# The last 64 features of the q/k/v products in float32r parts, and MLP weight rows split by ScalarE and GpSimd

## The chip, the cores and the metric

The kernel runs on one core of one Trainium2 chip. The metric is the device time of one execution in microseconds (us), read from the hardware; the kernel before took 3217.29 us (median of 3 runs, 3215.63 to 3218.51). The engines of the core are TensorE (PE in the profile; its weight loads are the row PEld), VectorE (DVE), ScalarE (ACT), GpSimd (POOL) and SyncE (SP), which only issues DMAs here. Each engine takes its instructions in one order; they meet through semaphores.

## The reference

One transformer block with conditioning, on x of 2 x 2048 x 576 in float32, with 16 heads of 36 and an MLP of 2304:

```python
mod = silu(c) @ w_ada + b_ada
sh_msa, sc_msa, g_msa, sh_mlp, sc_mlp, g_mlp = split(mod, 6, axis=1)
xn = ln(x, 1e-6) * (1 + sc_msa) + sh_msa
q, k, v = split(xn @ w_qkv + b_qkv)        # 576 -> 3 x 576
q, k = ln(q, 1e-5), ln(k, 1e-5)            # per head
o = softmax(q @ k.T * 36**-0.5) @ v
x = x + g_msa * (o @ w_proj + b_proj)
xn2 = ln(x, 1e-6) * (1 + sc_mlp) + sh_mlp
return x + g_mlp * (gelu(xn2 @ w1 + b1) @ w2 + b2)
```

The width of 576 matters for this change: it is four chunks of 128 rows and one of 64.

## The kernel before

The program first looks at the gains and biases of the head norms and then takes one of two branches; with these inputs it runs `block_of_small`. That branch goes through these stages, once for each of the two batches where not said otherwise:

1. **Inputs** (`inputs`, batch 0 from about 19 us, batch 1 from about 1110 us). For each of 16 tiles of 128 tokens: normalize the rows (`rows_normed`), turn them by five TensorE transposes (L357, L358), scale and shift them into `xnt` (L365), multiply by the weights of q, k and v, add the bias, normalize per head, and turn the result by nine transposes (L938) into `qo` and `kr`.
2. **Attention** (`attend`, L1073 and L1086 on TensorE, L1077 on ScalarE).
3. **Output projection** (`outputs`, from about 1038 us for batch 0 and 2121 us for batch 1). In the second of these, work for the MLP is laid between the tiles: `between` says at which tile t a piece is called. The pieces are the loads of the first token tiles, their norms, their transposes and shifts (`block_modulated`), and the preparation of w1.
4. **MLP**, first product (`whole_part` L1445, `last_part` L1459) and second product (L1610).

The q, k and v products each have two halves of 288 columns. A half is four matmuls with 128 rows (`whole`, L400) and one with 64 rows (`halved`, L411). The 64-row matmuls of the two halves sit in rows 0 to 63 and 64 to 127, so they run side by side; the transposed tail holds its 64 features twice, and `last_chunk` loads the weight rows accordingly. For most tiles the order on TensorE is q whole, transposes of the next tile, k whole, then three pairs of 64-row matmuls together, v whole, and the transposes by feature of two tiles ago. The last two tiles of a batch use `two_products`, which alternates the order of the two kinds.

The MLP's first product already treats its last 64 features differently. `last_modulated` writes the tail as a float32r part (L382), the tail in full (L383), and on GpSimd their difference (L384); `weight_parts` does the same to the weight rows on VectorE, with the high part in rows 0 to 63 and the remainder in rows 64 to 127 (L394, L395). Two float32r matmuls with all 128 rows (L1459), one for each part of the tokens, then give the product.

In the second output projection GpSimd's queue also issues the DMAs of the residual rows: `residual` loads a tile (L1178) and `summed` stores one (L1191). A load into one of the nine scratch tiles has to wait until the store of the tile that used it before is done. The w1 load of 4.7 MB (L1351) is issued by SyncE at the start of this stage.

TensorE's order is written out by hand throughout, VectorE's in the input stage, in attention and from the second output projection on, GpSimd's in attention. Elsewhere a scheduler sets the order when the program is built.

Of the kernel before, what the change touches and what calls it, by code (L numbers as in the profile page):

```python
# [8 lines left out]
F32 = mybir.dt.float32  # L9
F32R = mybir.dt.float32r  # L10
I32 = mybir.dt.int32
AF = mybir.ActivationFunctionType
# [19 lines left out]
def dit_block(  # L32
# [342 lines left out]

    def affine(which, k, b):
        return dict(bias=mod[:, which, k, b : b + 1], scale=mod[:, which + 1, k, b : b + 1])
# [8 lines left out]
    def modulated_parts(dst, cols, t4, t1, which, b):  # L386

        last_modulated(dst, cols, t1, which, b)
        for k in range(FULL):
            nc.scalar.activation(dst[0][:, k, cols], t4[:, k * P : (k + 1) * P], AF.Identity, **affine(which, k, b))  # L390

    def weight_parts(dst, src):

        nc.vector.tensor_copy(dst[0:64], src)  # L394
        nc.vector.tensor_tensor(dst[64:128], src, dst[0:64].bitcast(F32), ALU.subtract)  # L395
# [350 lines left out]
    def block_of_small():  # L746
# [10 lines left out]
        close_xs = token_tiles(5)  # L757
# [88 lines left out]
        def input_weights(then=lambda t: None):  # L846
            pool, close = opened("wq")
            wq = pool.tile([P, FULL, 3 * C], F32, name="wq")
            wq4 = pool.tile([P, 3, HALF], F32, name="wq4")
            bq = pool.tile([P, 3 * C], F32, name="bq")  # L850
            for f0, n in ((0, HALF), (HALF, HALF), (C, C), (2 * C, C)):
                f = slice(f0, f0 + n)
                nc.sync.dma_start(out=wq[:, :, f], in_=w_qkv[0:512, f].rearrange("(k p) f -> p k f", p=P))
                if f0 == HALF:
                    last_chunk(wq4, w_qkv, 3, HALF)
                if f0 == C:
                    then(1)
                    nc.sync.dma_start(out=bq, in_=b_qkv.partition_broadcast(P))
                    then(2)
            return (wq, wq4, bq), close  # L860
# [13 lines left out]
        def input_by_feature(b, rows, apart=False):  # L874
            xnt = xs["pool"].tile([P, NKC, P], F32, name="xnt", bufs=2)
            modulated(xnt, rows, 0, b, apart)
            return xnt

        def first_modulated():
            xnt = xs["pool"].tile([P, NKC, P], F32, name="xnt", bufs=2)  # L880
            for k in range(NKC):
                nc.scalar.activation(  # L882
                    xnt[:, k, :],
                    x_first[:, k * P : (k + 1) * P],
                    AF.Identity,
                    bias=mod[:, 0, k, 0:1],
                    scale=mod[:, 1, k, 0:1],
                )
            return xnt

        def inputs(b, weights, work, xnt, loaded):
# [75 lines left out]
            def next_rows(t):  # L967
                return tile_normed(loaded.pop(0)) if loaded else input_rows(b, t, nc.sync)

            def product(w, xnt):  # L970

                ps = s_tile()
                return ps, (
                    [ps[:, a, :HALF] for a in range(2)],
                    lambda k, a: xnt[:, k, :],
                    lambda k, a: (
                        wq[:, k, w * C + a * HALF : w * C + (a + 1) * HALF] if k < FULL else wq4[:, w, :]
                    ),
                )
# [16 lines left out]
            for t in range(NT - 2):  # L996
# [3 lines left out]
                q, q_parts = product(0, xnt)  # L1000
                whole(*q_parts, True)
                behind = b == t == 0
                if behind:
                    k, k_parts = product(1, xnt)
                    whole(*k_parts, True)
# [3 lines left out]
                rows = next_rows(t + 2)  # L1009
                if not behind:  # L1010
                    k, k_parts = product(1, xnt)
                    whole(*k_parts, True)
                v, v_parts = product(2, xnt)
                halved(*q_parts, False)
                halved(*k_parts, False)
                halved(*v_parts, True)
                biased(0, q, t, both)
# [3 lines left out]
                whole(*v_parts, False)  # L1021
# [7 lines left out]
            for t in range(NT - 2, NT):  # L1029
                both = work.tile([P, 2 * C], F32, name="both", bufs=3)  # L1030
                for w in range(3):
                    ps, parts = product(w, xnt)
                    two_products(*parts, 3 * t + w)
# [316 lines left out]
        for i, (k, f) in enumerate(((0, 0), (0, 1), (1, 0), (1, 1))):  # L1350
            nc.sync.dma_start(  # L1351
                out=wb[:, i],
                in_=w1[k * PAIR : (k + 1) * PAIR, f * MH : (f + 1) * MH].rearrange("(k p) f -> p k f", p=P),
            )
        weight_sums = [
            lambda: weight_parts(wr[0], last_rows[:, 0]),
            lambda: weight_parts(wr[1], last_rows[:, 1]),
            lambda: nc.vector.tensor_tensor(last_rows[:, 1], last_rows[:, 1], last_rows[:, 0], ALU.subtract),
            lambda: weight_parts(wr[2], last_rows[:, 1]),
# [25 lines left out]
        for i, t in enumerate((6, 7, 8, 9, 10, 11, 12, 14)):  # L1385
            between.setdefault(t, []).append(weight_sums[i])
        in_order = tc.manual_schedule(engines={mybir.EngineType.DVE})
# [310 lines left out]
```

## Time and profile before

| | |
|---|---|
| median of 3 runs | 3217.29 us |
| the profiled execution, its own time | 3216.58 us |
| its span, first to last instruction | 3214.8 us |
| TensorE busy | 3192.7 us, 99% of the span |
| ScalarE, VectorE, GpSimd busy | 1509.1, 1459.6, 369.1 us |
| weight loads | 1904.6 us, beside the matmuls |
| mean granted TensorE clock | 0.999 |

Durations and gaps in the text are from this one execution. A float32 matmul leaves two records on TensorE and a float32r matmul one, so "x16" of L400 is eight matmuls. The records of consecutive matmuls overlap; what one costs is read from start to start. In the timeline a row is: start in us from the beginning of the span, length in us, engine, line, operation, tiles written and read, shape, count, and in brackets how long the engine was idle before it and what ended that.

### The profile page before, as it was taken

Reading aid. Unit: us, or ns where it says so; the run is one execution under the profiler, and the core shown is the slowest. Engines: PE = TensorE matmul, PEld = TensorE weight load, DVE = VectorE, ACT = ScalarE, POOL = GpSimd, SP = SyncE. Lnnn points to the kernel's source line nnn. Section 1 sums busy time; section 2 is a strip of 40 time slices with the busy share of each in tenths; the row PEclk is TensorE's granted clock in tenths of the full one; section 3 lists DMA queues with packets and bytes.
Section 4 is the critical chain, followed back from the end, with each engine's and each line's share of the span. In section 5 each row is a group of like instructions: output and inputs, shape, how many; then the busy total and the mean of one; then the engine's idle time right before and its main releaser. Section 6 shows DMA issues by size and latency. Waiting matters only on the chain.

```text
span 3214.8 us, 47053 instructions
## 1 busy us (share of the span) xinstructions
PE 3192.7 (99%) x18143; PEld 1904.6 (59%) x18143; DVE 1459.6 (45%) x2137; ACT 1509.1 (47%) x2984; POOL 369.1 (11%) x464
## 2 busy tenths in 40 slices
PE   8999999999999999999999999999999999999999
PEld 6774333333333777633333333358888888777777
DVE  4674333333333367633333333345555444455454
ACT  2335666666666033466666666633555552000000
POOL 2111000112110111200001111011000000111111
PEclk9999999999999999999999999999999999999999
DMA  4102212223221401121222223144322223333321
GB/s 132 30 26 68 75 33 69 64 72 86 71 81 34 145 23 31 30 54 44 48 47 67 65 69 75 44 160 166 121 88 91 95 80 128 136 133 111 118 103 38
DMA packets 129172, 252.86 MB, mean 79 GB/s; under 512 B 22947, under 2 KB 68460, under 8 KB 126828
## 3 DMA queue, kind: packets, MB, share of 16 engines
q1 hardware_dynamic: 105428, 181.78, 18.6%
q0 software_dynamic: 22640, 66.23, 7.4%
q8 instruction: 145, 2.38, 0.3%
q10 hardware_dynamic: 872, 1.77, 0.2%
q14 instruction: 87, 0.71, 0.1%
HBM read 135.11 MB, written 66.35 MB: 63 GB/s over the span
## 4 chain that ended last, share of the span: by engine, by line
PE 98%; DMA 1%; DVE 0%; SPq 0%; issue 0%; ACT 0%; POOL 0%; DVEq 0%; POOLq 0%
PE b L1086 28%; PE b L1073 19%; PE s L1610 15%; PE s L400 15%; PE m L1445 12%; PE m L1459 2%; PE s L411 2%; PE one L1445 2%; PE s L938 1%; PE s L357 0%; PE t L1505 0%; DMA wq<-in_w_qkv_dram 0%; DMA x_dram<-x 0%; PE b L192 0%; PE b L938 0%
## 5 line engine op out<-in xcount | busy, mean ns | idle before, releaser
L1077 ACT ACTIVATE pt<-b 128x512 f32<-128x512 f32 x2048 | 1057.7, 610 | 485.3 <-PE b L1086 272.2
L1086 PE MATMUL b<-pt,vt 128*64 128x512 f32 x4096 | 935.0, 599 | 0.0
L1086 PEld LDWEIGHTS b<-pt,vt 128*64 128x64 f32 x4096 | 272.0, 136 | 581.8 <-issue 439.2
L1073 PE MATMUL b<-qm,km 32*128 32x512 f32 x4096 | 566.9, 614 | 0.2 <-DMA km<-qo 0.2
L1134 DVE TENSOR_TENSOR ot<-b,ot 128x512 f32<-128x512 f32 x192 | 132.8, 692 | 652.9 <-PE b L1086 652.5
L1073 PE MATMUL b<-qe,ke 16*128 16x512 f32 x2048 | 423.1, 790 | 0.0
L400 PE MATMUL s<-wq,xnt 128*128 128x288 f32 x1536 | 391.4, 409 | 1.2 <-ACT xnt L882 0.8
L1610 PE MATMUL s<-ws,as 128*128 128x288 f32 x1440 | 351.8, 406 | 0.0
L1073 PEld LDWEIGHTS b<-qm,km 32*128 32x128 f32 x4096 | 191.8, 185 | 269.1 <-ACT pt L1077 207.0
L400 PEld LDWEIGHTS s<-wq,xnt 128*128 128x128 f32 x1536 | 285.1, 190 | 85.4 <-issue 13.5
L1610 PEld LDWEIGHTS s<-ws,as 128*128 128x128 f32 x1440 | 274.1, 190 | 75.1
L1105 DVE RECIPROCAL den<-den 128x512 f32<-128x512 f32 x64 | 213.6, 3337 | 10.8 <-DMA den<-den_dram 10.8
L1445 PE MATMUL m<-s,wb 128*128 128x256 f32 x864 | 210.1, 380 | 0.2 <-DVE s L1415 0.2
L1445 PE MATMUL m<-xnt,wb 128*128 128x256 f32 x864 | 210.2, 379 | 0.0
L1132 DVE COPY ot<-b 128x512 f32<-128x512 f32 x64 | 44.3, 692 | 334.7 <-PE b L1086 334.7
L1445 PEld LDWEIGHTS m<-s,wb 128*128 128x128 f32 x864 | 164.4, 190 | 22.5 <-DVE s L1415 0.6
L1073 PEld LDWEIGHTS b<-qe,ke 16*128 16x128 f32 x2048 | 108.3, 184 | 114.2 <-issue 112.8
L1445 PEld LDWEIGHTS m<-xnt,wb 128*128 128x128 f32 x864 | 159.1, 190 | 18.7
L1472 DVE TENSOR_TENSOR cs<-m,cs 128x512 f32<-128x512 f32 x72 | 49.8, 691 | 215.8 <-PE m L1459 207.1
L1610 PE MATMUL s<-ws,hidden 128*128 128x288 f32 x576 | 142.3, 406 | 0.0
L1588 DVE TENSOR_TENSOR as<-hidden 128x1152 f32<-128x1152 f32 x80 | 139.2, 1803 | 0.0
L400 PE MATMUL s<-wp,qo 128*128 128x288 f32 x512 | 127.8, 410 | 0.0
(182 smaller groups left out, 2573.9 us busy)
## 6 DMA issues: line engine op xcount, KB each, us to landing
gelu<-cs SPq DMA_DIRECT2D x144, 256.0 KB
hidden<-gelu SPq DMA_DIRECT2D x16, 2304.0 KB
den<-den_dram SPq DMA_DIRECT2D x128, 128.0 KB
x_dram<-kr POOLq DMA_DIRECT2D x48, 288.0 KB, 2.8
qm<-qo SPq DMA_DIRECT2D x192, 64.0 KB
kr<-in_x_dram POOLq DMA_DIRECT2D x32, 288.0 KB, 3.8
xr<-x_dram SPq DMA_DIRECT2D x32, 288.0 KB
out_dram<-y POOLq DMA_DIRECT2D x30, 288.0 KB, 3.8
```

What stands on the lines that cost most here:

```text
L400: nc.tensor.matmul(outs[a], stationary(k, a), moving(k, a), start=(first and k == 0), stop=(not first and k == FULL - 1),)
L411: nc.tensor.matmul(outs[a], stationary(FULL, a)[r], moving(FULL, a)[r], start=first, stop=not first)
L1073: nc.tensor.matmul(ps, k[r, keys], q[r, :], start=first, stop=not first)
L1077: nc.scalar.activation(pt[:, h, :], banks[2 * c + h], AF.Exp, scale=SCALE)
L1086: nc.tensor.matmul(acc[64 * h : 64 * h + 64, :], vt[:, v0 : v0 + 64], pt[:, h, :], start=pt is pts[0][0], stop=pt is pts[-1][0],)
L1105: nc.vector.reciprocal(den, den)
L1134: nc.vector.tensor_tensor(ot, acc, ot, ALU.add)
L1445: nc.tensor.matmul(out_m[m], wb[:, slot[m], k, f * P : (f + 1) * P], moving[m](k), start=k == 0 and m in (1, 2, 5, 6), stop=k == 1 and m == 1,
L1459: nc.tensor.matmul(out_m[m], wr[w][:, f * P : (f + 1) * P], a[:, i, t * PAIR : (t + 1) * PAIR], start=False, stop=i == 1 and m != 2,)
L1472: nc.vector.tensor_tensor(cs[:, 0:5:4, :], two(1), cs[:, 4:5, :].to_broadcast([P, 2, PAIR]), ALU.add)
L1588: nc.vector.tensor_tensor(stationary[m], x_, y_, op)
L1610: nc.tensor.matmul(ms[m], stationary[m][:, f, :], ws[m][:, f, :], start=(f == 0), stop=(f == HF - 1))
```

## The change

In the input stage the 64-row pairs go. `xnt` becomes a tuple of a tile with the four full chunks, a float32r tile with two parts, and a tail; each half of a product is now four float32 matmuls followed by two float32r matmuls with 128 rows. `product` runs both halves at once, so that q, k and v are each completed before the next begins, and the biases follow at once. The tail's weight rows are loaded into the first 64 rows of `bq`, split from there by VectorE, and only then is the bias loaded into `bq`. The parts of the tail are written after the four full chunks instead of before them. The pool of token tiles shrinks from five to four.

For the MLP, the split of w1's last rows moves: ScalarE makes the copy and GpSimd the subtraction, also of the sum of the two column halves. The four sums of `wb` stay on VectorE. They are called at tiles 6, 8, 10 and 12 instead of 10, 11, 12 and 14, and the pieces on the other two engines at 7, 9, 11 and 13 instead of 6 to 9.

```diff
+    def part_tiles(pool, cols, **bufs):
+        return (
+            pool.tile([P, FULL, cols], F32, name="xnt", **bufs),
+            pool.tile([P, 2, cols], F32R, name="xnt4", **bufs),
+            pool.tile([P, P], F32, name="tail", bufs=1),
+        )
...
     def modulated_parts(dst, cols, t4, t1, which, b):
-        last_modulated(dst, cols, t1, which, b)
         for k in range(FULL):
             nc.scalar.activation(dst[0][:, k, cols], t4[:, k * P : (k + 1) * P], AF.Identity, **affine(which, k, b))
-
-    def weight_parts(dst, src):
-        nc.vector.tensor_copy(dst[0:64], src)
-        nc.vector.tensor_tensor(dst[64:128], src, dst[0:64].bitcast(F32), ALU.subtract)
+        last_modulated(dst, cols, t1, which, b)
+
+    def weight_parts(dst, src, subtract=None):
+        if subtract is None:
+            nc.vector.tensor_copy(dst[0:64], src)
+        else:
+            nc.scalar.copy(dst[0:64], src)
+        (subtract or nc.vector).tensor_tensor(dst[64:128], src, dst[0:64].bitcast(F32), ALU.subtract)
...
-        close_xs = token_tiles(5)
+        close_xs = token_tiles(4)
...
-            wq4 = pool.tile([P, 3, HALF], F32, name="wq4")
+            wq4 = pool.tile([P, 3 * C], F32R, name="wq4")
...
                 if f0 == HALF:
-                    last_chunk(wq4, w_qkv, 3, HALF)
+                    nc.sync.dma_start(out=bq[0:64, :], in_=w_qkv[512:576, :])
+                    weight_parts(wq4, bq[0:64, :])
...
         def input_by_feature(b, rows, apart=False):
-            xnt = xs["pool"].tile([P, NKC, P], F32, name="xnt", bufs=2)
-            modulated(xnt, rows, 0, b, apart)
+            xnt = part_tiles(xs["pool"], P, bufs=2)
+            t4, t1 = transposed(*rows, apart)
+            modulated_parts(xnt, slice(0, P), t4, t1[:, :P], 0, b)
             return xnt
...
             def product(w, xnt):
                 ps = s_tile()
-                return ps, (
-                    [ps[:, a, :HALF] for a in range(2)],
-                    lambda k, a: xnt[:, k, :],
-                    lambda k, a: (
-                        wq[:, k, w * C + a * HALF : w * C + (a + 1) * HALF] if k < FULL else wq4[:, w, :]
-                    ),
-                )
+                full, parts, _ = xnt
+                for a in range(2):
+                    f = slice(w * C + a * HALF, w * C + (a + 1) * HALF)
+                    out_a = ps[:, a, :HALF]
+                    for k in range(FULL):
+                        nc.tensor.matmul(out_a, full[:, k, :], wq[:, k, f], start=k == 0, stop=False)
+                    for i in range(2):
+                        nc.tensor.matmul(out_a, parts[:, i, :], wq4[:, f], start=False, stop=i == 1)
+                return ps
...
-                q, q_parts = product(0, xnt)
-                whole(*q_parts, True)
+                q = product(0, xnt)
                 behind = b == t == 0
                 if behind:
-                    k, k_parts = product(1, xnt)
-                    whole(*k_parts, True)
+                    k = product(1, xnt)
                 ahead = input_by_feature(b, rows, t in ((0, 9), (0, 1))[b])
                 rows = next_rows(t + 2)
+                biased(0, q, t, both)
                 if not behind:
-                    k, k_parts = product(1, xnt)
-                    whole(*k_parts, True)
-                v, v_parts = product(2, xnt)
-                halved(*q_parts, False)
-                halved(*k_parts, False)
-                halved(*v_parts, True)
-                biased(0, q, t, both)
+                    k = product(1, xnt)
                 biased(1, k, t, both)
                 if t > 0:
                     head_scale(t - 1, before)
-                whole(*v_parts, False)
+                v = product(2, xnt)
                 biased(2, v, t, both)
...
+        left, right = last_rows[:, 0], last_rows[:, 1]
+        last_parts = [
+            lambda: weight_parts(wr[0], left, nc.gpsimd),
+            lambda: weight_parts(wr[1], right, nc.gpsimd),
+            lambda: nc.gpsimd.tensor_tensor(right, right, left, ALU.subtract),
+            lambda: weight_parts(wr[2], right, nc.gpsimd),
+        ]
         weight_sums = [
-            lambda: weight_parts(wr[0], last_rows[:, 0]),
-            lambda: weight_parts(wr[1], last_rows[:, 1]),
-            lambda: nc.vector.tensor_tensor(last_rows[:, 1], last_rows[:, 1], last_rows[:, 0], ALU.subtract),
-            lambda: weight_parts(wr[2], last_rows[:, 1]),
             lambda: nc.vector.tensor_tensor(wb[:, 4], wb[:, 1], wb[:, 0], ALU.subtract),
...
-        for i, t in enumerate((6, 7, 8, 9, 10, 11, 12, 14)):
+        for i, t in enumerate((6, 8, 10, 12)):
             between.setdefault(t, []).append(weight_sums[i])
+            between.setdefault(t + 1, []).append(last_parts[i])
```

More of the change, by code (lines that the diff above doesn't have):

```diff
@@ L874, in input_by_feature @@
         def input_by_feature(b, rows, apart=False):
-            xnt = xs["pool"].tile([P, NKC, P], F32, name="xnt", bufs=2)
-            modulated(xnt, rows, 0, b, apart)
+            xnt = part_tiles(xs["pool"], P, bufs=2)
+            t4, t1 = transposed(*rows, apart)
+            modulated_parts(xnt, slice(0, P), t4, t1[:, :P], 0, b)
             return xnt
         def first_modulated():
[L880 to L887, printed above, removed]
-                )
+            xnt = part_tiles(xs["pool"], P, bufs=2)
+            modulated_parts(xnt, slice(0, P), x_first[:, :512], x_first[:, 512:], 0, 0)
             return xnt
@@ L972, in product @@
                 ps = s_tile()
-                return ps, (
-                    [ps[:, a, :HALF] for a in range(2)],
-                    lambda k, a: xnt[:, k, :],
-                    lambda k, a: (
-                        wq[:, k, w * C + a * HALF : w * C + (a + 1) * HALF] if k < FULL else wq4[:, w, :]
-                    ),
-                )
+                full, parts, _ = xnt
[7 more added lines that the diff above has]
+                return ps
             def biased(w, ps, t, both):
@@ L1031, in inputs @@
                 for w in range(3):
-                    ps, parts = product(w, xnt)
-                    two_products(*parts, 3 * t + w)
+                    ps = product(w, xnt)
                     biased(w, ps, t, both)
```

## The prediction

> **What bounds the kernel now.** I read the page's chain first: work on TensorE all the way.
>
> ```profile
> PE 98%; DMA 1%; DVE 0%; SPq 0%; issue 0%; ACT 0%; POOL 0%; DVEq 0%; POOLq 0%
> ```
>
> So the change counts where it alters TensorE's work or makes it wait. Next, the timeline of one token tile in the input stage, TensorE alone:
>
> ```profile
> 118.50 4.15 PE L400 MATMUL s<-wq,xnt 128*128 128x288 f32 x16
> 122.49 1.15 PE L938 MATMUL s<-ident,both 128*128 128x128 f32 x9
> 123.47 4.05 PE L400 MATMUL s<-wq,xnt 128*128 128x288 f32 x16
> 127.35 0.60 PE L357 MATMUL s<-ident,xt 128*128 128x128 f32 x4
> 127.79 0.27 PE L358 MATMUL s<-ident,xt 128*128 128x128 f32 x1
> 127.90 4.05 PE L400 MATMUL s<-wq,xnt 128*128 128x288 f32 x16
> 131.88 1.73 PE L411 MATMUL s<-wq,xnt 64*128 64x288 f32 x12
> 133.53 1.24 PE L400 MATMUL s<-wq,xnt 128*128 128x288 f32 x4
> ```
>
> Start to start, without a gap: 133.53 - 118.50 = 15.03 us per tile. A float32 record of 288 columns costs 3.88/16 = 0.2425 us (123.47 to 127.35). The three 64-row pairs take 1.65 us where two records each make 3 x 0.485 = 1.455, and the L400 blocks on either side of them take 3.98 and 3.99, not 3.88: some 0.4 us per tile goes at the borders between 128-row and 64-row matmuls. Then the nearest rows for the new operations, in the MLP's first product:
>
> ```profile
> 2226.20 1.03 PE L1445 MATMUL m<-s,wb 128*128 128x256 f32 x4
> ...
> 2227.06 1.03 PE L1445 MATMUL one<-xnt,wb 128*128 128x256 f32 x4
> 2227.74 1.30 PE L1459 MATMUL m<-parts,wr 128*128 128x256 f32 x8
> 2228.88 0.27 PE L1505 MATMUL t<-ident,xt 128*128 128x128 f32 x1
> ```
>
> Four float32 records take 0.86 us; from 2227.06 to 2228.88 are 1.82, so the eight float32r matmuls take 0.96, 0.120 each, and no border shows. Last, the timeline of the second output projection, where the moved pieces stand:
>
> ```profile
> 2151.93 0.54 POOL L1178 DMA_DIRECT2D x<-x_dram  x1 [8.87 <-DMA x_dram<-x]
> ...
> 2155.26 0.29 ACT L276 ACTIVATE std<-mv,eps 128x1 f32<-128x1 f32 x1 [3.40 <-DVE mv L274]
> ...
> 2157.18 0.60 PE L357 MATMUL s<-ident,xt 128*128 128x128 f32 x4
> ...
> 2161.22 0.54 POOL L1178 DMA_DIRECT2D x<-x_dram  x1 [5.76 <-DMA x_dram<-x]
> ...
> 2163.89 0.46 ACT L383 ACTIVATE tail<-s,mod 128x128 f32<-128x128 f32 x1 [5.51 <-POOL parts L384]
> ...
> 2171.10 1.12 PE L357 MATMUL s<-ident,xt 128*128 128x128 f32 x4 [3.32 <-DVE product L1183]
> ...
> 2181.07 0.60 PE L357 MATMUL s<-ident,x_first 128*128 128x128 f32 x4
> ```
>
> GpSimd's queue stands still for DMA stores, ScalarE's behind it, and TensorE loses 3.3 us at 2171.
>
> **What the skill says.** The Trainium skill, "TensorE: Matmul & The Clock Gate", section "Back-to-back issue gap", gives N/2.4 + 2.5 ns for a warm matmul: 122.5 ns at 288 columns; the trace's 0.120 at 256 columns is above its 109. The same page, "What's actually happening", says that an idle TensorE falls to half clock for some 3.4 us: after the gap at 2171.10 the same 5 transposes and 32 records take 9.97 us to the next start, where 0.545 + 32 x 0.2425 = 8.31 are due; so 1.66 us is lost. "Architectural detail" on that page calls ScalarE's and VectorE's queues strict FIFO, as the 5.51 us above show. "GPSIMD Engine Reference", section "Elementwise — side-by-side cycle accounting", has 4497 ns for a two-input operation on 2048 elements; the trace's L1166 takes 1416 ns for 576 and L384 452 for 128, 2.15 ns per element.
>
> **The input stage.** Removed per tile: 1.455 us of 64-row pairs and 0.4 of borders. Added: 12 float32r matmuls. I take 0.122 each, the skill's figure and half a float32 record; the low end is the measured 0.120, the high end 0.133, should the 13 ns by which 0.120 exceeds 256 columns at 0.2425/576 per column be fixed. New tile: 48 x 0.2425 = 11.64, 14 transposes 1.53 (0.98 + 0.55), 1.46, and 0.03 for handing back to float32: 14.66, a gain of 0.37. For 27 tiles: 10.0. The last two tiles of a batch take 29.99 (228.66 to 258.65; 1318.11 to 1348.10) and need 96 x 0.2425 + 23 x 0.109 + 24 x 0.122 + 0.06 = 28.8: 1.2 per batch, 2.4. That leaves batch 0's first tile. VectorE is free at 19.4; the split of 64x1728 scales from L394 (744 ns at 1152) and L395 (1351) to 1.04 + 1.95, so the parts exist at 22.5. TensorE, starting at 18.90, wants them at 20.84 and waits 1.7. From there 0.24 + 1.94 + 0.24 (q), 4.37 (k), 0.55, 4.37 (v): the next tile starts at 34.2. Before, it is also 34.2, after waits for weights at 23.45 and 30.31. The bias load now waits for the split, and v's weights stand behind it on SP: 0.885 + 1.18 MB at 397 GB/s from 23.5 are there at about 29.5, needed at 29.9. No gain, and 0 to 1 us of loss; I take 0.3. Sum: **-12.1 us**, or -7.7 at 0.133.
>
> At nothing I cost: one more shift on ScalarE and a 0.45 us subtraction on GpSimd per tile (a tile's parts are wanted over 11 us after its transposes, ScalarE is busy 53 of 155 us there, and in the built order the subtraction stands before the scaling L928 of its iteration); four token tiles instead of five (a load may still start about two tiles ahead); the split for batch 1 (3 us on VectorE, whose next eviction TensorE awaits some 8 us later; without that cover, up to 3 us).
>
> **The second output projection.** VectorE loses 3 x (0.74 + 1.35) + 1.34 = 7.6 us, hidden but for part of the 3.3 us. What counts is where the built program puts the pieces. GpSimd: load x1_2 (the one at 2161.22), subtraction for wr1, load x1_3, difference of the halves, a store, the first tail subtraction. ScalarE: the copies for wr0 and wr1 before the first tile's square root, and the copy for wr2 **before the second tile's square root** (the one at 2155.26). That copy needs the difference, which needs GpSimd past the load at 2161.22. Behind the square root wait VectorE (its norm, then evictions) and TensorE's transposes of 2157.18. So: 2161.22 + 0.54, + 2.65 (1152 elements: 1416 + 576 x 2.15), + 0.54, + 2.65 = 2167.6; copy 1.16 (L913 has 1152 ns for that length); root 0.3; reciprocal, scaling and hops 0.9: transposes at 2170.0, 12.8 us late. With 1.7 of slow clock: +14.5. The old stall then goes, for the evictions are long ready: -(3.38 + 1.66) = -5.0. Net **+9.5 us**. Ends: GpSimd at L928's 2.13 us gives +8.5; at 1.84 times the price, the worst of L1593 (2607 for 576), +14; nothing or less only if that store lands 13 us sooner, while w1's 4.7 MB hold the DMA engines (DMA share 1.02 from 2140 to 2160). The copies for wr0 and wr1 delay the first tile's root by about 5 us; TensorE has about that much slack, and the later wait covers the rest.
>
> **Sum.** Against the profiled execution's 3216.6: -12.1 + 9.5 = 3214.0. It lies 0.7 below the median, so 3214.7 as a median; -2.6 us. No change means within 0.2%, 6.4 us, which is about what a measurement of this kernel can tell.
>
> **Rivals.**
> *The stall is hidden* (0.15): stores return sooner, the difference is ready early, and only the input stage and the old stall's end count: 3217.3 - 12.1 - 5 = 3200; half hidden, 3207. For it: DMA times are the least certain link. Against it: the load of w1 is untouched.
> *Slower, by the float32r matmuls* (0.17): row L1459 of the page is 91.0 us for 576, 158 ns each. Should they cost that when they alternate with float32 in twos, the stage gains 384 x 0.036 = 13.8 less, that is loses 1.7, and with the stall the time is 3217.3 + 1.7 + 9.5 = 3228. It decides at 0.129 each: above that the kernel is slower than before. Against it: 91.0 includes overlap with the float32 matmul ahead, and the starts give 0.120. For it: no trace shows pairs of them with 288 columns.
> *A second pass*: float32r of 288 columns at the float32 record's 0.2425 would cost 46 us, 3261 (0.03); L1459 speaks against it.
>
> **How the numbers follow.** Both effects as worked out: 0.65, 3209 to 3221. Faster 0.2 is the hidden stall and 0.05 of the forecast's tail, slower 0.2 the two dearer float32r prices, same the other 0.6. The range, 3205 to 3224, takes in 0.133 with the dear GpSimd price (3217.3 - 7.7 + 14 = 3223.6) and a stall half hidden (3207).
>
> **What would show it.** Tiles of the input stage 14.66 us apart without a 64-row matmul; TensorE waiting about 1.7 us at 21 us; in the second output projection a TensorE gap of some 13 us before the second tile's transposes, ScalarE's copy for wr2 released by GpSimd, and no gap at the third. It is wrong if tiles are over 14.8 us apart, if other gaps of a microsecond open in the input stage, or if that gap is under 8 or over 17 us.

## The result, and the profile after

The changed kernel takes 3226.47 us (median of 8 runs, 3225.47 to 3228.88), the kernel before beside it 3217.47 (8 runs, 3215.63 to 3218.51): a ratio of 1.003, 95% interval 1.0019 to 1.0041. It is 9.0 us slower; the prediction had it 2.6 us faster, and the time lies 2.5 us above the end of its range. The profiled execution took 3225.47 us with a span of 3223.7, 8.9 longer than before's 3214.8, so one pair of traces can be set against each other. TensorE still carries the chain of the page, but less of it:

```profile
PE 96%; DVE 1%; DMA 1%; issue 0%; ACT 0%; SPq 0%; POOL 0%; DVEq 0%; POOLq 0%; ACTq 0%
```

The stages, each from TensorE's first matmul of it to that of the next, in us:

| stage | before | after | difference |
|---|---|---|---|
| up to the first product | 18.90 | 20.04 | +1.14 |
| inputs, batch 0 | 239.76 | 237.96 | -1.80 |
| attention, batch 0 | 779.02 | 780.32 | +1.30 |
| output projection, batch 0 | 72.04 | 72.04 | 0 |
| inputs, batch 1 | 238.40 | 233.90 | -4.50 |
| attention, batch 1 | 772.75 | 772.95 | +0.20 |
| output projection, batch 1 | 79.12 | 91.74 | +12.62 |
| MLP, both products | 1014.82 | 1014.73 | -0.09 |

The input side was to bring 12.1 us and brought 3.7; the second output projection was to cost 9.5 and cost 12.6.

First the timeline of a token tile in the input stage, TensorE alone, half of v first:

```profile
119.19 2.10 PE L984 MATMUL s<-wq,xnt 128*128 128x288 f32 x8
120.91 0.64 PE L986 MATMUL s<-wq,xnt 128*128 128x288 f32 x2
121.39 2.10 PE L984 MATMUL s<-wq,xnt 128*128 128x288 f32 x8
...
133.47 0.65 PE L986 MATMUL s<-wq,xnt 128*128 128x288 f32 x2
133.96 1.37 PE L984 MATMUL s<-wq,xnt 128*128 128x288 f32 x5
```

The same place one tile later is 14.77 us on (119.19 to 133.96), not 14.66. A half takes 121.39 - 119.19 = 2.20; eight float32 records at 0.2425 are 1.94, so two float32r matmuls take 0.265, 0.1325 each.

The start of batch 0, TensorE alone before the change:

```profile
18.90 4.12 PE L400 MATMUL s<-wq,xnt 128*128 128x288 f32 x16 [0.76 <-ACT xnt L882]
...
27.43 0.60 PE L357 MATMUL s<-ident,xt 128*128 128x128 f32 x4
```

And after it, timeline of all engines:

```profile
19.18 0.26 PE L312 MATMUL s<-ident,gb_rows 18*128 18x18 f32 x1 [1.08 <-DMA gb_rows<-rows_dram]
20.04 4.18 PE L984 MATMUL s<-wq,xnt 128*128 128x288 f32 x8 [0.60 <-ACT xnt L397]
...
20.83 1.05 DVE L403 CAST wq<-bq 64x1728 fp32r<-64x1728 f32 x1
...
21.91 2.09 DVE L406 TENSOR_TENSOR wq<-bq,wq 64x1728 fp32r<-64x1728 f32 x1
...
24.15 0.82 PE L986 MATMUL s<-wq,xnt 128*128 128x288 f32 x2
...
24.77 2.71 PE L984 MATMUL s<-wq,xnt 128*128 128x288 f32 x8
...
31.99 0.60 PE L357 MATMUL s<-ident,xt 128*128 128x128 f32 x4
```

Eight records take 4.1 us instead of 1.94: TensorE had half its clock from about 19.2 to 26.0 us (PEclk, the share of its clock that it was granted, is 0.50 there; before the change it is 1.00 in these microseconds). The first float32r pair follows the end of the split (21.91 + 2.09 = 24.0), and the second tile's transposes come at 31.99, before at 27.43. Before, the first tile's 64-row matmuls and v still followed them, and now only v does; so the start of the second tile's products is the fairer measure: 36.94, before 34.30.

The end of batch 0's input stage, TensorE's only waits there:

```profile
239.18 2.21 PE L984 MATMUL s<-wq,xnt 128*128 128x288 f32 x8 [0.67 <-DVE both L992]
...
259.73 0.77 PE L1073 MATMUL b<-qm,km 32*128 32x512 f32 x3 [0.61 <-DVE vt L995]
```

In the last two tiles VectorE is late with the evictions: between 251 and 260 us it has one idle moment, of 0.46 us, as before the change. Attention's first exponential starts at 261.01, before at 260.27, although TensorE got to attention 0.65 us sooner: it waited 1.10 us for the scores, and these waited for the eviction of v (the 0.61 above), which they did not before.

And the second output projection, timeline of all engines:

```profile
2158.38 0.55 POOL L1178 DMA_DIRECT2D x<-x_dram  x1 [3.70 <-DMA x_dram<-x]
2158.95 2.62 POOL L406 TENSOR_TENSOR wr<-last_rows,wr 64x1152 fp32r<-64x1152 f32 x1
2161.50 0.55 POOL L1178 DMA_DIRECT2D x<-x_dram  x1
2162.11 2.60 POOL L1359 TENSOR_TENSOR last_rows<-last_rows 64x1152 f32<-64x1152 f32 x1
...
2164.74 1.15 ACT L405 CAST wr<-last_rows 64x1152 fp32r<-64x1152 f32 x1 [16.35 <-POOL last_rows L1359]
...
2165.80 0.29 ACT L276 ACTIVATE std<-mv,eps 128x1 f32<-128x1 f32 x1
...
2166.24 2.60 POOL L406 TENSOR_TENSOR wr<-last_rows,wr 64x1152 fp32r<-64x1152 f32 x1
2166.32 2.84 DVE L279 TENSOR_SCALAR xt<-xt,mv,rstd 128x576 f32<-128x576 f32 x1
...
2169.30 1.09 PE L357 MATMUL s<-ident,xt 128*128 128x128 f32 x4 [15.45 <-DVE xt L279]
...
2181.68 0.55 PE L357 MATMUL s<-ident,xt 128*128 128x128 f32 x3
```

The chain is the predicted one: a residual load held up by a store, subtraction, load, difference, ScalarE's third copy, the square root, the tile's scaling, TensorE. Only one link is new: VectorE's scaling took 2.84 us beside GpSimd's subtraction for wr2. Before, it took 0.58:

```profile
2155.79 0.58 DVE L279 TENSOR_SCALAR xt<-xt,mv,rstd 128x576 f32<-128x576 f32 x1
```

The gap is 15.45 us. The third tile's transposes (2181.68) no longer wait.

### The profile page after: what moved, and what is told of

Same layout as the page of the kernel before. It is cut to its first block, busy times and chain, and to the rows that moved or that the text cites. A ratio compares the mean times of both kernels' runs of the same rounds, so it can differ in the third digit from the quotient of the medians.

```text
span 3223.7 us, 47140 instructions
## 1 busy us (share of the span) xinstructions
PE 3188.8 (99%) x18143; PEld 1926.5 (60%) x18143; DVE 1458.4 (45%) x2134; ACT 1523.6 (47%) x3019; POOL 394.0 (12%) x500
## 4 chain that ended last, share of the span: by engine, by line
PE 96%; DVE 1%; DMA 1%; issue 0%; ACT 0%; SPq 0%; POOL 0%; DVEq 0%; POOLq 0%; ACTq 0%
PE b L1086 28%; PE b L1073 19%; PE s L1614 15%; PE m L1449 12%; PE s L984 11%; PE s L411 3%; PE m L1463 2%; PE one L1449 2%; PE s L986 1%; PE s L944 1%; PE s L357 0%; PE t L1509 0%; PE s L422 0%; DMA x_dram<-x 0%; DMA wa<-in_w_ada_dram 0%
## 5 line engine op out<-in xcount | busy, mean ns | idle before, releaser
L984 PE MATMUL s<-wq,xnt 128*128 128x288 f32 x1536 | 406.6, 408 | 1.3 <-DVE both L992 0.7
L1449 PEld LDWEIGHTS m<-xnt,wb 128*128 128x128 f32 x864 | 158.8, 190 | 18.9
```

Source lines behind the costliest of these rows:

```text
L984: nc.tensor.matmul(out_a, full[:, k, :], wq[:, k, f], start=k == 0, stop=False)
L1449: nc.tensor.matmul(out_m[m], wb[:, slot[m], k, f * P : (f + 1) * P], moving[m](k), start=k == 0 and m in (1, 2, 5, 6), stop=k == 1 and m == 1,
```

## The experiments

Theory Q says that the second output projection's loss comes of ScalarE's third copy queued behind GpSimd. Theory S puts the missing gain of the input side on the first tile of batch 0. The other questions are the price of a float32r matmul and what GpSimd does to VectorE. Runs of one group share the runs of the kernel before.

### Each part alone

e1_rows_alone is the kernel before with the MLP weight rows' part; e2_products_alone is the changed kernel without it:

```diff
-            lambda: weight_parts(wr[0], left, nc.gpsimd),
...
-            between.setdefault(t + 1, []).append(last_parts[i])
...
+            lambda: weight_parts(wr[0], last_rows[:, 0]),
...
+        for i, t in enumerate((6, 7, 8, 9, 10, 11, 12, 14)):
```

(that is e2; e1 makes the same edit the other way round in the kernel before).

> The kernel before with the MLP weight rows' split alone (ScalarE copies, GpSimd subtracts, new places); the input stages are those of before. Theory Q (the second output projection's loss comes of ScalarE's third copy queued behind GpSimd): that stage takes 91 to 93 us instead of 79.1, no other stage moves, and the time is 3229 to 3231 us, 12 to 13 above before. Rival I (the loss needs both parts of the change: the products' part shifts the order or the buffers, so that the split alone is cheap): the stage stays under 85 us and the time under 3223 us.

> The changed kernel with the MLP weight rows split on VectorE again, at their old places. Theory Q: the second output projection is back at 79 us, and what is left is the gain of the input stages less the loss at the start: 3213 to 3215 us, 2.5 to 4.5 under before. Rival I: the stage keeps a wait of 5 us or more and the time is above 3217 us. A second rival (the input stages gained nothing, the traces' difference of stages is chance): within 1 us of before, 3216.5 to 3218.5 us.

Measured: e1 3229.77 us against 3217.53 (ratio 1.0038, 1.0024 to 1.0052), the stage 90.77, just under the 91 expected; e2 3215.96 (0.9995, 0.9987 to 1.0004), the stage 80.78. So the loss belongs to the rows' part alone and does not need the products, and theory Q has the size. In e1 the scaling is slow again, beside the subtraction, and TensorE's gap was 15.05:

```profile
2170.88 2.60 POOL L398 TENSOR_TENSOR wr<-last_rows,wr 64x1152 fp32r<-64x1152 f32 x1 [0.20 <-ACT wr L397]
...
2171.22 2.57 DVE L279 TENSOR_SCALAR xt<-xt,mv,rstd 128x576 f32<-128x576 f32 x1
```

e2 gained 1.6 us, less than expected, and the interval includes no change at all. Its start shows where part of the gain went, TensorE alone:

```profile
19.17 2.18 PE L984 MATMUL s<-wq,xnt 128*128 128x288 f32 x8 [0.65 <-ACT xnt L397]
23.77 0.50 PE L986 MATMUL s<-wq,xnt 128*128 128x288 f32 x2 [2.42 <-DVE wq L406]
24.11 3.79 PE L984 MATMUL s<-wq,xnt 128*128 128x288 f32 x8
```

Here the clock is full at first, so the wait for the split is seen: 2.42 us. After it eight records take 3.3 us instead of 1.94, at half clock. The first input stage took 239.23 us, 0.5 less than before; the second 233.90, 4.5 less.

### The third copy, and the tail buffer behind it

e3_third_copy_on_gpsimd takes the copy off ScalarE's queue:

```diff
-            lambda: weight_parts(wr[2], right, nc.gpsimd),
+            lambda: (
+                nc.gpsimd.tensor_copy(wr[2][0:64], right),
+                nc.gpsimd.tensor_tensor(wr[2][64:128], right, wr[2][0:64].bitcast(F32), ALU.subtract),
+            ),
```

> The changed kernel with one edit: GpSimd makes the third copy too, so that ScalarE has nothing in its queue that waits for GpSimd ahead of the second tile's standard deviation. Theory Q: the gap of TensorE ahead of the second tile's transposes goes, and with it the lower clock after it; the stage takes 74 to 78 us (below before's 79.1 if before's gap at the third tile stays away too), and the time is 3209 to 3213 us. Rival G (GpSimd's own work is the bound: 2.6 us for each subtraction on a queue that also issues the rows' loads and stores): the gap moves but stays 8 us or more, the stage takes over 86 us, and the time is above 3220 us. VectorE's scaling of a tile (0.58 us alone, 2.84 beside a GpSimd subtraction in the changed kernel) is expected to take up to 2.6 us more wherever it meets a GpSimd instruction of this size.

Measured: 3220.96 us (1.0010, 1.0002 to 1.0018), the stage 85.57. The gap before the second tile went from 15.45 to 1.24 us, so the copy did cause it; but waits of 2.73 and 4.55 us stand before the third, where the kernel before had 3.32. Timeline of all engines there:

```profile
2160.82 4.80 DVE L1367 TENSOR_TENSOR wb<-wb 128x2304 f32<-128x2304 f32 x1 [3.56 <-DMA wb<-in_w_dram]
...
2163.73 4.36 POOL L1359 TENSOR_TENSOR last_rows<-last_rows 64x1152 f32<-64x1152 f32 x1
...
2168.62 0.47 POOL L392 TENSOR_TENSOR parts<-tail,parts 128x128 fp32r<-128x128 f32 x1
...
2169.12 0.46 ACT L391 ACTIVATE tail<-s,mod 128x128 f32<-128x128 f32 x1 [9.74 <-POOL parts L392]
```

ScalarE has a second wait for GpSimd's queue: there is one tail buffer per block, and the small subtraction that frees it stands behind the large ones. It is the 5.51 us of the kernel before, grown to 9.74. And VectorE's sum and GpSimd's difference slowed each other, 4.80 for 2.55 and 4.36 for 2.60. Neither expectation was met whole.

Two tail buffers take the second wait away (e7 and e11; e9 gives the kernel before one such buffer, which both blocks share):

```diff
+                mx.tile([P, P], F32, name=f"other_tail{i}"),
...
-            modulated_parts(to, slice(i * P, (i + 1) * P), t4, t1[:, :P], 2, b)
+            modulated_parts((to[0], to[1], to[2 + i % 2]), slice(i * P, (i + 1) * P), t4, t1[:, :P], 2, b)
```

> e3_third_copy_on_gpsimd with the two tail buffers alone added (its first tile as in the changed kernel). Theory T (once the third copy is off its queue, ScalarE's 9.74 us for the tail buffer are what is left of the wait on GpSimd): the third tile's square root comes 2.5 us sooner or more, and the stage takes 76 to 80 us instead of 85.6, the time 3211 to 3215.5 us. Rival C (VectorE and GpSimd slow each other where both read two operands of SBUF, 4.80 for 2.55 us and 4.36 for 2.60 there, and that is the larger part): the stage stays above 82 us, the time above 3217.5 us.

> The changed kernel with the two tail buffers alone; ScalarE's third copy stays where it is. Theory Q (the third copy's wait for GpSimd is the larger part): the gap ahead of the second tile's transposes stays at 14 to 16 us, the stage takes 89 to 92 us instead of 91.7 and the time is 3224 to 3227 us. Rival T2 (the tail buffer alone would do): the stage takes under 84 us and the time is under 3219 us.

> The kernel before with one edit: a second tail buffer, which odd tiles of the MLP's blocks take. Theory T: the old stall is nothing but ScalarE waiting for the tail buffer, so the second output projection falls from 79.1 to 74 to 75 us and the time to 3212 to 3213 us, whatever becomes of the q/k/v products. Compared with e6_and_two_tails (3211.2), this tells what the products' change is worth by itself, its start mended: theory S expects 1 to 3 us. A rival (the products' change is worth 5 us or more once the stall is away) would have 3216 us or more here.

| stage, us | one tail buffer | two |
|---|---|---|
| rows on VectorE, products of before | 79.12 (before) | 74.14 (e9) |
| rows on VectorE, products changed | 79.87, 80.78 (e5, e2) | 74.54 (e6) |
| GpSimd copies and subtracts | 85.57 (e3) | 81.67 (e7) |
| ScalarE copies, GpSimd subtracts | 91.74 (changed) | 94.04 (e11) |

e7 3217.25 us (1.0000, 0.9991 to 1.0008); e11 3229.17 (1.0035, 1.0022 to 1.0049), its gap still 16.55 and the time above what was expected; e9 3213.84 against 3217.08 (0.9989, 0.9982 to 0.9995), just above the 3212 to 3213 expected. In e9 ScalarE's tail no longer waits, and the 3.3 us gap at the third tile is gone, with that one edit:

```profile
2160.22 0.45 ACT L383 ACTIVATE other_tail<-s,mod 128x128 f32<-128x128 f32 x1
...
2169.66 0.66 PE L357 MATMUL s<-ident,xt 128*128 128x128 f32 x4
```

With the copy in ScalarE's queue the buffer does nothing (e11); once it is out, the buffer is worth 3.9 us (e3 to e7). The stage comes out above the 76 to 80 us expected and just under rival C's 82. What is left in e7 against e6 is 7.1 us, and the two traces account for it. Counted from the start of the stage, the second tile's transposes come 3.2 us later. From there to the next 64-row matmuls TensorE takes 11.37 us instead of 8.40, at half clock for part of it. From the third tile's transposes to the fourth's it takes 0.95 longer. The largest gap, in the timeline of all engines, is:

```profile
2156.05 2.61 POOL L406 TENSOR_TENSOR wr<-last_rows,wr 64x1152 fp32r<-64x1152 f32 x1
...
2156.32 2.65 DVE L279 TENSOR_SCALAR xt<-xt,mv,rstd 128x576 f32<-128x576 f32 x1
...
2159.12 1.09 PE L357 MATMUL s<-ident,xt 128*128 128x128 f32 x4 [3.42 <-DVE xt L279]
```

The scaling follows its reciprocal without a wait, and yet it ends only after the subtraction has ended.

### VectorE beside GpSimd

e8_side_by_side measures that alone, on weights that are no longer read:

```diff
+                    for _ in range(2):
+                        V.tensor_tensor(d1, d0, d1, ALU.subtract)
+                    for _ in range(2):
+                        V.tensor_scalar(d1, d1, bq[:, 0:1], bq[:, 1:2], ALU.subtract, ALU.mult)
+                    for _ in range(2):
+                        V.tensor_tensor(d1[:, :HALF], ps[:, 0, :HALF], d1[:, :HALF], ALU.add)
+                    for _ in range(2):
+                        V.tensor_copy(d1, d0)
+                    for _ in range(2):
+                        V.tensor_reduce(d1[:, 0:1], d0, AX.X, ALU.add)
...
+                for _ in range(8):
+                    G.tensor_tensor(p1, p0, p1, ALU.subtract)
+                vector_round()
```

> The changed kernel with instructions of no use after batch 1's last input tile, on 128 x 1152 float32 of the weights, which are no longer read: on VectorE two each of a subtraction of two SBUF operands, a scaling by two per-row numbers, an addition with a PSUM operand (288 columns), a copy and a sum over columns, first alone and then beside eight GpSimd subtractions. Theory P (VectorE's faster one-operand forms and its two-operand forms share a way to SBUF with GpSimd and its other forms do not): beside GpSimd the scaling and the copy stretch to the end of the GpSimd instruction under way (up to 2.6 us more), the two-operand subtraction takes some 1.9 times its time and so do GpSimd's beside it; the addition with a PSUM operand and the sum over columns keep their time to 5%. Rival D (everything on VectorE slows alike, by the SBUF traffic): the sum over columns slows as well, by 50% or more.

Alone, then (from 1361.45) beside eight GpSimd subtractions, which take 2.61 alone; each row is two instructions:

```profile
1349.87 1.79 DVE L1063 TENSOR_SCALAR wq<-wq,bq 128x1152 f32<-128x1152 f32 x2
1351.77 0.95 DVE L1065 TENSOR_TENSOR wq<-s,wq 128x288 f32<-128x288 f32 x2
1352.75 1.55 DVE L1067 COPY wq<-wq 128x1152 f32<-128x1152 f32 x2
1354.34 2.74 DVE L1069 TENSOR_REDUCE wq<-wq 128x1 f32<-128x1152 f32 x2
...
1361.49 25.20 POOL L1077 TENSOR_TENSOR wq<-wq 128x1152 f32<-128x1152 f32 x8 [0.28 <-DVE wq L1075]
1366.52 6.13 DVE L1063 TENSOR_SCALAR wq<-wq,bq 128x1152 f32<-128x1152 f32 x2
1372.69 0.95 DVE L1065 TENSOR_TENSOR wq<-s,wq 128x288 f32<-128x288 f32 x2
1373.67 5.17 DVE L1067 COPY wq<-wq 128x1152 f32<-128x1152 f32 x2
...
1378.88 2.74 DVE L1069 TENSOR_REDUCE wq<-wq 128x1 f32<-128x1152 f32 x2
```

The scaling goes from 0.88 to 3.05 us each, the copy from 0.76 to 2.08 and 3.07, a subtraction of two SBUF operands from 1.36 to 3.65 (the second of its pair; the first began 0.04 us ahead of GpSimd and kept its 1.36, while GpSimd's took 3.78). The addition with a PSUM operand and the sum over columns do not move. Theory P holds in what slows and what does not, though not in every size: the subtraction takes 2.7 times its time instead of 1.9, GpSimd's 1.4 times. Rival D falls. The Trainium skill, "SBUF — State Buffer", section "SBUF: two separate sides", says just this: VectorE's two-port performance modes, which a float32 copy triggers, and its operations with two SBUF inputs share a pair of ports with GpSimd, whoever starts first holds it for the whole instruction, and "the other fully blocks". This case's traces agree, with 0.58 against 2.57 to 2.84 us for the same scaling.

### The price of a float32r matmul

e4_float32r_chains appends chains whose results are not read:

```diff
+                def small(cols, i):
+                    nc.tensor.matmul(ps[:, 0, :cols], parts[:, i % 2, :], wq4[:, :cols], start=True, stop=True)
...
+                for cols in (128, 256, 288, 384, 512):
+                    for i in range(24):
+                        small(cols, i)
```

> The changed kernel with chains of products of no use added after the last input tile of batch 0, their result unread: 24 float32r products each of 128, 256, 288, 384 and 512 columns, 24 float32 each of 256 and 288, then six times (four float32, two float32r) and six times (two float32, one float32r) of 288 columns. Theory F (every float32r product costs a fixed time over its columns: 12.5 ns, from 0.120 us at 256 and 0.1325 at 288 columns[...]): 0.066, 0.119, 0.1325, 0.1725 and 0.226 us apart; the mixed chains cost the sum of their members, 4 x 0.2425 + 2 x 0.1325 = 1.235 us a turn. Rival B (the border between the two types costs it, a chain of one type runs at 0.120 for 288 columns): 0.053, 0.107, 0.120, 0.160, 0.213 us apart, and the mixed chains are dearer than the sum by 0.025 us a turn. Rival L (loading 128 rows of weights in float32r sets a floor): 128 and 256 columns cost the same, about 0.12 us.

From the first start of a chain to that of the next (261.521, 264.148, 266.943, 270.138, 274.333, 279.923), over 24; and from one start to the next once a chain runs evenly, without the first few of it:

| columns | 128 | 256 | 288 | 384 | 512 |
|---|---|---|---|---|---|
| float32r, us each | 0.109 | 0.116 | 0.133 | 0.175 | 0.233 |
| in an even chain | 0.112 | 0.113 | 0.133 | 0.175 | 0.233 |
| theory F | 0.066 | 0.119 | 0.1325 | 0.1725 | 0.226 |

Float32 records took 0.2158 at 256 columns and 0.2425 at 288. A mixed turn, TensorE alone:

```profile
303.65 0.64 PE L994 MATMUL s<-wq,xnt 128*128 128x288 f32 x2
304.13 2.10 PE L997 MATMUL s<-wq,xnt 128*128 128x288 f32 x8
305.85 0.64 PE L994 MATMUL s<-wq,xnt 128*128 128x288 f32 x2
```

It takes 2.20 us, the sum of its members (8 x 0.2425 + 2 x 0.1325 = 2.205), so there is no border cost: rival B falls. Theory F had the value at 288 right and the law wrong. From 288 columns on the price is near proportional, 0.455 to 0.463 ns per column (0.133/288, 0.233/512), not a fixed addition. At 128 and 256 columns it is the same within 2%, 0.112 and 0.113: the floor that rival L had. What sets it was not tried.

### The first tile

Four edits, each on top of the one before. The products' part alone with batch 0's first tile in the old order (e5):

```diff
-                q = product(0, xnt)
+                q = product(0, xnt, small=not behind)
...
-                    k = product(1, xnt)
+                    k = product(1, xnt, small=False)
...
                 rows = next_rows(t + 2)
+                if behind:
+                    product(0, xnt, q, large=False)
+                    product(1, xnt, k, large=False)
```

(`large` and `small` say whether a product issues its float32 and its float32r matmuls); the two tail buffers shown above (e6); the load of the last 64 weight rows first (e10):

```diff
+            nc.sync.dma_start(out=bq[0:64, :], in_=w_qkv[512:576, :])
             for f0, n in ((0, HALF), (HALF, HALF), (C, C), (2 * C, C)):
...
                 if f0 == HALF:
-                    nc.sync.dma_start(out=bq[0:64, :], in_=w_qkv[512:576, :])
                     weight_parts(wq4, bq[0:64, :])
```

and the bias load last (e12):

```diff
                     then(1)
-                    nc.sync.dma_start(out=bq, in_=b_qkv.partition_broadcast(P))
                     then(2)
+            nc.sync.dma_start(out=bq, in_=b_qkv.partition_broadcast(P))
```

> The products' part alone (as in e2_products_alone) with one edit: batch 0's first tile goes in the order of before, the four whole chunks of q and of k first, then the second tile's transposes, and only then the float32r products of both. Theory S (the wait of TensorE for the split of the weight rows, 2.42 us in e2_products_alone, and the half clock after it took the input stage's gain of batch 0): no wait for the split is left, the first input stage takes 235.5 to 236.5 us instead of 239.2, and the time is 3212 to 3214 us, 2.5 to 4 under e2_products_alone's 3216.0. Rival V (the bias load and v's weights, which stand behind the split on SP, are what the first tile waits for): v's product waits instead, the stage stays above 238 us and the time above 3215 us.

> e5_first_tile_order with one edit more: the MLP's token tiles take two tail buffers in turn, so that ScalarE need not wait for GpSimd's subtraction of the tile before (5.51 us in the kernel before, ahead of TensorE's 3.3 us at the third tile). Theory T (that wait is the root of the old stall): the gap before the third tile's transposes goes, the second output projection takes 75 to 76.5 us instead of 80.8, and the time is 4 to 5 us under e5_first_tile_order, 3207.5 to 3210 us. Rival E (VectorE's and GpSimd's own work in that stage makes the third tile late anyway): a gap of 2 us or more stays and the time is within 2 us of e5_first_tile_order.

> e6_and_two_tails with the load of the last 64 feature rows of the q/k/v weights put ahead of the four large loads instead of after two of them. Theory V (what is left of the first tile's loss is v's weights and the bias, queued on SP behind the split): the split ends 1.2 to 1.6 us sooner, v's product waits 0 to 0.5 us instead of 1.67, and the time is 0.5 to 1.5 us under e6_and_two_tails' 3211.2. Rival H (what is left is TensorE's half clock after its own wait at 18 to 20 us, which comes of the small rows' load landing late): nothing changes, within 0.7 us of 3211.2; the 32 records of q and k take over 9 us where the gap ahead of them is over 1.5 us.

> e10_rows_first with the bias load moved behind v's weights on SP, so that only the bias waits for the split of the weight rows and v's weights do not. Theory V (the first tile's last loss is v's weights, held on SP behind the split): the DMA engines, 0.43 busy at 24 to 26 us in e10_rows_first, stay near 1.0 there; v's product, which waited 2.46 us, waits 0.5 us or less; the first input stage takes 235 to 236.5 us instead of 238.1 and the time is 1.5 to 2.5 us under e10_rows_first's 3209.8, 3207.3 to 3208.3. Rival W (the bias, now last, is what q's eviction waits for, and v's product waits for the eviction's PSUM buffer as long as before): v's product still waits 1.5 us or more and the time is within 0.7 us of 3209.8.

| run | time, us | ratio to before | first input stage | second output projection |
|---|---|---|---|---|
| e2 | 3215.96 | 0.9995 (0.9987 to 1.0004) | 239.23 | 80.78 |
| e5 | 3215.03 | 0.9994 (0.9986 to 1.0003) | 237.23 | 79.87 |
| e6 | 3211.16 | 0.9982 (0.9974 to 0.9989) | 239.57 | 74.54 |
| e10 | 3209.80 | 0.9978 (0.9968 to 0.9988) | 238.08 | 74.41 |
| e12 | 3209.64 | 0.9973 (0.9962 to 0.9984) | 237.31 | 75.44 |

In e5 TensorE no longer waits for the split, but the time fell by 0.9 us where 2.5 to 4 were expected, and not beyond the scatter. e6 did what theory T said of the stage; its time, 3.9 us under e5, is above the 3207.5 to 3210 expected, which were reckoned from a faster e5. e10's time, 1.4 us under e6, is as theory V had it, its mechanism not: the split ended only 0.7 us sooner (24.26 against 24.99), and v's product waited longer, 2.46 us. The gain may as well be the clock, as rival H has it: q's and k's 32 records took 10.6 us in e6's trace, after waits of 2.15 and 0.59 us with one small matmul between them, and 8.3 in e10's after one of 0.66. The cause of the 2.46 us shows in e10's windows of 2 us (the last columns are PEclk, DMA share and GB/s):

```profile
22.00:24.00 2.00, 2.00 (x10) 1.58 (x9) 1.97 (x2) 0.54 (x2) 1.38 (x1) 1.00 0.82 304
24.00:26.00 2.00, 1.83 (x8) 1.16 (x7) 0.59 (x2) 0.00 (x0) 0.58 (x1) 1.00 0.43 75
```

The DMA engines fall to 0.43 busy: the bias load on SP waits for the split, and v's weights behind it. With the bias last (e12), the same two windows and v's start:

```profile
22.00:24.00 2.00, 2.00 (x6) 1.41 (x5) 1.77 (x1) 0.00 (x0) 0.00 (x0) 0.53 1.05 388
24.00:26.00 2.00, 2.00 (x10) 1.58 (x9) 1.37 (x5) 0.29 (x1) 0.00 (x0) 1.00 1.06 393
```

```profile
31.66 2.21 PE L984 MATMUL s<-wq,xnt 128*128 128x288 f32 x8 [0.43 <-ACT xnt L397]
```

The transfer goes on and v waits 0.43 us. So theory V's mechanism is there and rival W's is not. But the time did not follow, 3209.64, nor the stage, 237.31 where 235 to 236.5 were expected: this trace has half clock before 24 us, e10's did not. Half clock at the start also shows in e1 and e9, whose input stage is that of before, after gaps of 0.79 us. When it comes, and why the first product starts anywhere from 19.2 to 20.8 us with the changed products and from 18.9 to 19.9 with those of before, stays open.

## Why the prediction was wrong, point by point

**Its direction.** Both mechanisms were there, but the input side was worth 3.7 us and not 12.1, the stall 12.6 and not 9.5.

**The tiles, -10.0.** The step that failed is the price of a float32r matmul. The trace's own row gave 0.120 at 256 columns; scaled with the columns that is 0.135. The prediction took 0.122, half a float32 record, and measured is 0.1325, its named high end. e4 shows that neither is a law: 128 and 256 columns cost the same there. That gives 0.25 instead of 0.37 per tile, and the starts of the tiles show it: from the second tile to the fifteenth 3.3 us were gained in batch 0 (34.30 to 228.66 before, 36.94 to 227.99 after), and from the first to the fifteenth 3.6 in batch 1 (1109.71 to 1318.11, 1110.36 to 1315.18). Together that is 6.9 us over the 27 tiles, 3.1 short. The prediction's own boundary of 0.129, above which the change costs more than it brings, was passed; the rival's 0.158 and its border were not there.

**The first tile, +0.3.** The second tile's products start 2.6 us later, at 36.94 instead of 34.30. Two terms failed. The split was to end at 22.5 and ended at 24.0, which is 1.5: "VectorE is free at 19.4" was read from the trace of before, while here its small work ahead of the split ended at 20.74, behind a small matmul (19.18 above) that had waited for its load. The first product was 1.1 us later as well, but within the wait for the split. And the clock was taken as full, though the prediction priced half clock in the other stage: from the end of the split to 26.0 us it was half, which costs another 1.0. With these two and 0.0105 more for each float32r matmul the prediction's own sum gives 36.8. In e2, where the clock is full at first, the wait shows as 2.42 us (1.7 predicted). v's weights, which the prediction had in time, came in time here too, but with luck: DMA share was 0.54 at 24 to 26 us where it had counted on 397 GB/s from 23.5 on (which makes 28.7, not 29.5), and the products that need them were late themselves.

**The last two tiles, -2.4.** From the start of the fifteenth tile to attention's first exponential it was -0.6 in batch 1 (31.61 to 31.00) and +1.4 in batch 0 (31.61 to 33.02), together 3.2 us worse than predicted. The prediction summed TensorE's work and left out that VectorE's evictions set this stretch. With e4's chains put in ahead of attention, which give VectorE time to finish, batch 0's attention took 778.89 us, as before the change. Why batch 0 is worse than batch 1 was not tried.

**What was costed at nothing** for the steady tiles cost nothing: ScalarE, GpSimd and four token tiles show no wait there.

**The second output projection, +9.5.** The transposes came 15.8 us late, not 12.8: measured from the start of the stage the load was 0.8 later, and the scaling 2.26 longer. From there the half clock cost 1.83 (1.7 predicted: 10.23 us from the transposes to the next start against 8.40), and the old stall's 5.04 went, as predicted; 15.76 + 1.83 - 5.04 = 12.55. The failed step here is "scaling and hops": it was priced from a row where GpSimd stood still, while the change itself set a 2.6 us subtraction beside it. The queue was right in every other link (e1, e3).

**The range.** Its top of 3224 took in two dear ends at once, -7.7 for the input side and +14 for the stall. The stall stayed inside its end; the input side did not, for the first tile and the last two came on top. None of the signs by which the prediction was to be wrong appeared: the tiles are 14.77 us apart, no wait in the input stage reaches a microsecond, and the gap is 15.45. They watched the two main effects and not the ends of the stage.

## What to carry to other kernels

Before work goes to GpSimd, ask two things: who waits behind the engine that waits for it, and which VectorE instructions of two SBUF operands or of the fast one-operand kind will run beside it; here each of those stretched by up to GpSimd's length. A buffer that a waiting engine's queue must free is as much a dependence as data: a second tail buffer of 64 KB brought 3.2 us to the kernel before (e9), and one for each block 3.9 to the changed products (e5 to e6). That is about as much as the products' change itself, which comes to 2 to 5 us once its start is mended (e6, e10 and e12 against e9; their traces differ in the clock at the start). The best version, e12 at 3209.64 us (0.9973 of before, 0.9962 to 0.9984), not distinguishable from e10's 3209.80, has the changed products with the old order in the first tile, the rows on VectorE, two tail buffers, and loads in an order in which nothing waits for the split but the bias.

## What the runs showed of the hardware

- In e4 a float32r matmul of 128 rows and 128 weight columns took 0.455 to 0.463 ns per column from 288 columns on, and 112 and 113 ns at 128 and 256 columns, so that halving the width brought nothing there. A float32 record took 0.842 ns per column at 256 and 288; neither kind paid for following the other. The Trainium skill's N/2.4 + 2.5 ns ("TensorE: Matmul & The Clock Gate", "Back-to-back issue gap") gives 109, 122.5 and 216 ns at 256, 288 and 512 columns; measured are 113, 133 and 233, so the measurement decides for float32r.
- VectorE and GpSimd behaved as if they took turns: in e8 2.61 us of GpSimd beside VectorE became 3.0 to 3.8, and VectorE's 0.76 to 1.36 became 2.1 to 3.7, its scalings and copies ending 0.6 us after the GpSimd instruction that was under way when they began. Its sum over columns and its PSUM addition kept their 1.35 and 0.46.
- Half clock after a gap was not a matter of the gap alone: at the start the same 32 records took 8.3 us in e10 and 9.5 in e9 and e12, with a gap of 0.65 to 0.8 us ahead of them in all three. What else it depends on stays open.
